# Turning the adjacency on VectorE, by way of DRAM, instead of on TensorE in the first graph stage

## The chip, the cores and the metric

The kernel runs on one core of a Trainium2 chip. A core has five engines with instruction streams of their own: TensorE (PE in the profile) for matrix products, VectorE (DVE), ScalarE (ACT), GpSimd (POOL) and SyncE (SP), which here only issues DMAs. GpSimd issues DMAs too. The metric is the device time of one execution in microseconds, as a median of several runs; the time of a run is somewhat longer than the span that its profile shows.

## The reference

A two-layer graph network on x of 16 batches, 1024 nodes and 256 channels, with one adjacency `adj` of 1024 x 1024 for all batches. All data is float32. Cut to what matters:

```python
# layer 0, per batch; h = relu(layernorm(x)), fea = h transposed
c_adj = mean(fea, channels)
A = abs(abs(sigmoid(c_adj[None, :] - c_adj[:, None]) - 0.5) - 0.5) * 2   # symmetric
g = relu((fea @ (adj * A)) * para)               # "graph product", gives the queries
k, v = split(h @ kv_w)
x = x + softmax(q @ k.T * scale) @ v             # 4 heads of 64 channels
# layer 1; h = relu(layernorm(x))
A_norm = adj + eye
deg = A_norm.sum(0) + A_norm.sum(1) - diag(A_norm)
A_hat = A_norm * rsqrt(deg)[:, None] * rsqrt(deg)[None, :]
agg = A_hat @ h                                  # per batch
x = x + batchnorm(relu(batchnorm(agg @ W1.T + b1)) @ W2.T + b2)
```

Layer 0 reads the adjacency by rows. Layer 1 needs it transposed in the tile `ahatT`, scaled by the roots of the degrees. The transposed copy, the sums and the scaling are made once, while batch 0 is worked on.

## The kernel before

Nodes lie in 8 chunks of 128 partitions. `adj_t[0..7]` hold the rows of the adjacency for the whole run. Work of each engine is issued in the order of the program text, which is written out by hand: functions take lists of small steps ("hooks") that they call at set places, so an instruction's place in the text is its place in its engine's queue, SyncE's and GpSimd's DMA queues included. An engine that waits holds everything queued behind it.

Batch 0 begins with its layer norm. `prepare_row(0)` makes, by transposes on TensorE (L317, L323), a row of node means that is the same on every partition. `weights(b, c)` makes one chunk of masked weights: two activations on ScalarE (L350, L353) from the row, then one operation on VectorE with the adjacency chunk (L367). Weights sit in the pool `w4`, which has five buffers; the graph's parameters, W1 and W2 pass through the same five.

`graph(0, between)` runs over the 8 chunks: it calls the steps of `between[c]`, then multiplies (L489) into two PSUM tiles. At chunk 5 it loads the parameters (L482), whose buffers come free when chunks 3 and 4 have been multiplied. After the last chunk come seven products each for values and keys (`V.product`, `K.product`: a seven-product scheme with sums on VectorE, `add`, and copies on ScalarE, `copy`).

Among these steps stand the adjacency's eight blocks. `turn_adj(i)` and `turn_adj_aside(i)` transpose the eight 128 x 128 pieces of one row chunk on TensorE against the identity into PSUM (L1372, L1387), and `place_adj` copies the result into `ahatT` on VectorE, or once on ScalarE (L1378, L1393). `row_sums` and `column_sums` are activations with an accumulator on ScalarE. `diagonal` takes out the diagonal and adds the identity on GpSimd, 16 small operations, and reduces it on VectorE (L1414).

`prepare_row(b)` for later batches writes the means to DRAM in 4-byte pieces (`frow`, L312) and loads them back broadcast to all partitions (`f_row`, L313), both on SyncE. For batch 1 this is a step at the end of the chunks, `between[8]`.

`attention(0, ...)` then runs four steps. In each, `scores` makes 8 score tiles (L868, three PSUM buffers) with exponentials on ScalarE (L876) and sums on VectorE; before the last sum it calls `hooks[i]`. `partial` and `values` (L920) follow. `hooks[0]` and `hooks[1]` make batch 1's first two chunks of weights; column sums stand in all four hooks, two in each; `roots` in the last. In step 2 `collect`, `invert` and `spread` spread the reciprocals of the softmax's sums. After the attention comes `graph(1, ...)`, whose fourth chunk is preceded by `roots_row`, and then the scaling of `ahatT`. From there on the batches run alike.

[...]

Of the kernel before, what the change touches and what calls it, by code (L numbers as in the profile page):

```python
# [10 lines left out]
F32 = mybir.dt.float32  # L11
# [18 lines left out]
def fast_path(  # L30
# [39 lines left out]
    w2T_d = dram.tile([P, FC, C], F32, tag="fw2T", name="fw2T")  # L70
    w1s_d = dram.tile([P, 4, FC * P // 2], F32, tag="fw1s", name="fw1s")
# [106 lines left out]
    with ExitStack() as stage:  # L178
# [291 lines left out]
        def graph(b, between):  # L470
# [42 lines left out]
            if b == 0:  # L513
# [8 lines left out]
                K.copy(0, 0)  # L522
                V.product(6)
# [9 lines left out]
                K.copy(1, 0)  # L533
                V.product(4)
# [13 lines left out]
                K.copy(0, 1)  # L548
                return qT, kT, v
# [819 lines left out]
        def turn_adj(i):  # L1369
            ps = ps_s.tile([P, NC, P], F32, tag="s", name=f"f_adjps_{i}")  # L1370
            for m in range(NC):
                nc.tensor.transpose(ps[:, m, :], adj_t[i][:, ts(m, P)], ident)  # L1372
            turned_adj[i] = ps

        turned_adj = {}

        def place_adj(i, copy):
            copy(columns(i), turned_adj.pop(i).rearrange("p m (q i) -> p m i q", i=NC))  # L1378

        def turn_adj_aside(i):  # L1380

            turned_adj[i] = [
                ps_o.tile([P, NC // 2, P], F32, tag="o", name=f"f_adjpsa_{i}"),
                ps_t.tile([P, NC // 2, P], F32, tag="t", name=f"f_adjpsb_{i}"),
            ]
            for m in range(NC):
                nc.tensor.transpose(  # L1387
                    turned_adj[i][m // 4][:, m % 4, :], adj_t[i][:, ts(m, P)], ident
                )

        def place_adj_aside(i, copy):
            for n, ps in enumerate(turned_adj.pop(i)):
                copy(columns(i)[:, 4 * n : 4 * n + 4], ps.rearrange("p m (q i) -> p m i q", i=NC))  # L1393
# [14 lines left out]
        def diagonal():  # L1408
# [5 lines left out]
            nc.vector.tensor_reduce(diag, on, AX.X, ALU.add)  # L1414
# [44 lines left out]
        with tc.manual_schedule(engines={ENG.PE, ENG.Activation, ENG.DVE, ENG.Pool, ENG.SP}):  # L1459
# [16 lines left out]
            turn_adj(0)  # L1476
            place_adj(0, nc.vector.tensor_copy)
            xs[1] = load_x(1)
            prepare_row(0)
            turn_adj(1)  # L1480
            turn_adj_aside(2)
            place_adj(1, nc.vector.tensor_copy)
# [5 lines left out]
            def load_w1T():  # L1488
# [6 lines left out]
                    1: [  # L1495
                        lambda: place_adj_aside(2, nc.vector.tensor_copy),
# [39 lines left out]
            for b in range(B):  # L1536

                hooks, aside, behind = {}, {}, None
                if b + 1 < B:
# [9 lines left out]
                    if b == 0:  # L1549
                        for m in range(NC):  # L1550
                            hooks.setdefault(m // 2, []).append(lambda m=m: column_sums(m))
# [985 lines left out]
```

## Time and profile before

| | us |
|---|---|
| median of 3 runs (lowest, highest) | 2359.56 (2359.32, 2362.05) |
| the profiled execution's own time | 2359.85 |
| its span | 2358.1 |
| TensorE busy in the span | 2319.4 |
| VectorE busy | 1994.5 |
| ScalarE busy | 1416.2 |
| GpSimd busy | 447.5 |
| first graph product, start | 16.58 |
| first product of keys and values, start | 48.72 |
| first scores of batch 0, start | 61.07 |
| first graph product of batch 1, start | 117.41 |

A timeline row has a start, a duration, the engine, the line, the operation with the tiles that it writes and reads, and a count when equal instructions are merged; in brackets the idle time of the engine before it and what ended it. A float32 matrix product of 512 columns counts as two matrix instructions. Starts are in microseconds from the start of the span. In the kernel after the change lines are shifted: those behind the new `adjT_d` by 1, those of the attention by 7.

### The profile page before, as it was taken

The page shows a single profiled execution, that of the slowest core. Times are in us where ns is not written, and L with a number is a line of the kernel's source. Part 1 is how long each engine was busy: PE and PEld are TensorE (multiplying, and loading weights), DVE is VectorE, ACT ScalarE, POOL GpSimd, SP SyncE. Part 2 cuts the span into 40 slices and gives each one's busy share as a digit, 9 for nine tenths or more (in the row PEclk, how much of TensorE's full clock was granted, in tenths as well). Part 3 has the DMA queues.
Part 4 walks back from the last instruction along what each step waited for, and adds up shares of the span by engine and source line. Part 5 has one row for each costly group of instructions (what it writes and reads, how often), then busy time and mean ns, then how long its engine had stood idle before and what let it go on. Part 6 is the DMA issues. An engine that isn't in the chain of part 4 may idle for free.

```text
span 2358.1 us, 25774 instructions
## 1 busy us (share of the span) xinstructions
PE 2319.4 (98%) x8256; PEld 1030.5 (44%) x8256; DVE 1994.5 (85%) x2937; ACT 1416.2 (60%) x2057; POOL 447.5 (19%) x573
## 2 busy tenths in 40 slices
PE   8999999999999999999999999999999999999995
PEld 5353444434353434444343434343444434444444
DVE  7988989898989899897989798988989898757766
ACT  6846556574838465655657384746556575346644
POOL 5121212112221112221212221222212121100000
PEclk9999999999999999999999999999999999999998
DMA  6143443524342434335343324253343421355579
GB/s 205 46 143 99 139 138 117 161 107 122 130 138 69 170 96 162 115 134 143 113 132 132 123 86 156 90 179 99 134 143 116 156 77 54 128 215 176 171 243 380
DMA packets 169217, 326.42 MB, mean 138 GB/s; under 512 B 34928, under 2 KB 102000, under 8 KB 169072
## 3 DMA queue, kind: packets, MB, share of 16 engines
q1 hardware_dynamic: 145264, 268.02, 33.3%
q0 software_dynamic: 19200, 39.88, 6.3%
q10 hardware_dynamic: 4608, 16.78, 1.7%
q8 instruction: 67, 1.10, 0.2%
q14 instruction: 78, 0.64, 0.1%
HBM read 203.96 MB, written 101.77 MB: 130 GB/s over the span
## 4 chain that ended last, share of the span: by engine, by line
PE 97%; DMA 1%; DVE 1%; issue 0%; ACT 0%; SPq 0%; ACTq 0%; POOLq 0%; POOL 0%; DVEq 0%
PE f_s L868 19%; PE f_o L920 19%; PE f_aps L1085 16%; PE f_gps L686 8%; PE f_zps L1195 7%; PE f_gpsx L686 6%; PE f_zx L1756 4%; PE f_zm L1756 3%; PE f_gps L489 2%; PE f_vpsx L433 2%; PE f_kpsx L428 2%; PE f_vps L433 2%; PE f_kps L428 2%; PE f_z2ps L1694 1%; PE f_zps L1278 1%; PE f_zps3a L1195 1%
## 5 line engine op out<-in xcount | busy, mean ns | idle before, releaser
L876 ACT ACTIVATE f_p<-f_s 128x1024 f32<-128x1024 f32 x512 | 477.0, 1047 | 59.8 <-PE f_s L868 59.8
L868 PE MATMUL f_s<-f_qT,f_kT 64*128 64x512 f32 x2048 | 456.8, 596 | 0.0
L920 PE MATMUL f_o<-f_p,f_v 128*64 128x512 f32 x2048 | 453.6, 595 | 0.0
L868 PEld LDWEIGHTS f_s<-f_qT,f_kT 64*128 64x128 f32 x2048 | 191.2, 185 | 263.6 <-issue 118.3
L920 PEld LDWEIGHTS f_o<-f_p,f_v 128*64 128x64 f32 x2048 | 141.4, 137 | 304.4 <-issue 265.7
L363 POOL TENSOR_TENSOR f_w<-f_w,f_adj 128x1024 f32<-128x1024 f32 x56 | 132.2, 2362 | 700.9 <-ACT f_w L362 506.7
L988 POOL DMA_DIRECT2D f_att<-f_oT x256 | 136.1, 539 | 342.8 <-DVE f_oT L971 337.3
L891 DVE TENSOR_TENSOR f_acc<-f_acc,f_p 128x1024 f32<-128x1024 f32 x128 | 156.0, 1219 | 4.6 <-ACT f_p L876 4.6
L891 DVE TENSOR_TENSOR f_sums<-f_sums,f_p 128x1024 f32<-128x1024 f32 x128 | 155.9, 1218 | 0.0
L350 ACT ACTIVATE f_w<-f_row,f_col 128x1024 f32<-128x1024 f32 x127 | 147.4, 1160 | 10.9 <-DMA f_row<-frow 4.6
L353 ACT ACTIVATE f_w<-f_w 128x1024 f32<-128x1024 f32 x127 | 134.4, 1058 | 4.0
L1085 PE MATMUL f_aps<-f_ahatT,f_hs 128*128 128x512 f32 x256 | 115.1, 592 | 0.0
L1085 PE MATMUL f_aps<-f_ahatT,f_h_b 128*128 128x512 f32 x256 | 112.6, 593 | 0.0
L1085 PE MATMUL f_aps<-f_t,f_hs 128*128 128x512 f32 x256 | 112.5, 592 | 0.0
L362 ACT ACTIVATE f_w<-f_w,f_now 128x1024 f32<-128x1024 f32 x56 | 64.3, 1148 | 78.9 <-DVE f_now L360 78.9
L686 PE MATMUL f_gps<-f_w,f_h_a 128*128 128x512 f32 x224 | 109.8, 592 | 0.0
L882 DVE TENSOR_TENSOR f_acc<-f_p,f_p 128x1024 f32<-128x1024 f32 x64 | 77.9, 1218 | 24.9 <-ACT f_p L876 24.9
L888 DVE TENSOR_TENSOR f_sums<-f_p,f_p 128x1024 f32<-128x1024 f32 x64 | 78.2, 1221 | 20.2 <-ACT f_p L876 20.1
L367 DVE SCALAR_TENSOR_TENSOR f_w<-f_w,f_adj 128x1024 f32<-128x1024 f32 x71 | 88.0, 1258 | 7.5 <-ACT f_w L353 7.4
L283 ACT ACTIVATE f_h_a<-f_x,f_shift_a,f_rstd_a 128x256 f32<-128x256 f32 x126 | 73.8, 587 | 32.3 <-DVE f_shift_a L268 32.3
L1218 ACT ACTIVATE f_z<-f_zps,f_b 128x512 f32<-128x512 f32 x60 | 38.0, 683 | 75.3 <-PE f_zps L1195 75.3
L283 ACT ACTIVATE f_h_b<-f_x,f_shift_b,f_rstd_b 128x256 f32<-128x256 f32 x128 | 66.2, 592 | 25.8 <-DVE f_shift_b L268 25.8
(297 smaller groups left out, 3984.2 us busy)
## 6 DMA issues: line engine op xcount, KB each, us to landing
f_t<-ft SPq DMA_DIRECT2D x84, 512.0 KB, 9.7
fz<-f_z SPq DMA_DIRECT2D x64, 512.0 KB, 9.5
f_x<-in_x_dram SPq DMA_DIRECT2D x31, 1024.0 KB, 6.2
f_zb<-fz SPq DMA_DIRECT2D x42, 512.0 KB, 4.6
fx<-f_x SPq DMA_DIRECT2D x16, 1024.0 KB, 4.4
fgs<-f_gs POOLq DMA_DIRECT2D x28, 512.0 KB, 3.0
fhT<-f_hQ POOLq DMA_DIRECT2D x112, 128.0 KB, 3.2
f_hT<-fhT SPq DMA_DIRECT2D x28, 512.0 KB, 6.4
```

What stands on the lines that cost most here:

```text
L283: nc.scalar.activation(self.h[:, c, :], self.xt[:, c, :], AF.Relu, bias=self.shift[:, c : c + 1], scale=self.rstd[:, c : c + 1], accum_out ...
L350: nc.scalar.activation(w, rows[b], AF.Abs, bias=cols[b][:, c : c + 1], scale=0.5 / C)
L353: nc.scalar.activation(w, w, AF.Tanh)
L686: nc.tensor.matmul(ps, left, right, start=fresh and n == 0, stop=(n == PAIRS - 1), skip_group_check=more,)
L868: nc.tensor.matmul(ps[:, e, :], kT[rows_e, pair, ts(m, P)], qT[rows_e, pair, ts(g, 512)], start=True, stop=True,)
L876: nc.scalar.activation(p, ps, AF.Exp)
L891: nc.vector.tensor_add(to, to, p)
L920: nc.tensor.matmul(o_of[s][e * HD : (e + 1) * HD, :], v[:, m, ts(2 * pair + e, HD)], p[:, e, :], start=(m == 0), stop=(m == NC - 1),)
L988: queue.dma_start(t[ts(j, 32), :, a].rearrange("r h c i -> r h (c i)"), oT[ts(a, 32), :, j].rearrange("r h c i -> r h (c i)"),)
L1085: nc.tensor.matmul(ps, left[:, m, :], right(m), start=not more and m == 0, stop=(m == KH - 1), skip_group_check=more,)
L1195: nc.tensor.matmul(ps[i], left[:, ts(i, P)], right, start=not more, stop=True, skip_group_check=more,)
L1756: nc.tensor.matmul(ps, left[:, m, :], right[:, m, :], start=start and m == 0, stop=(m == 1), skip_group_check=not start,)
```

## The change

The transposes on TensorE and the copies out of PSUM go. The adjacency is loaded a second time, its rows sorted so that VectorE's transposition of 32 x 32 blocks, done on eight tiles of 128 x 1024, leaves in `ahatT` (as a staging area) pieces that eight stores from GpSimd's queue put in DRAM as the transposed matrix (`adjT_d`, pieces of 512 bytes). Four loads of 1 MB bring it back into `ahatT`.

The 32 loads of 128 KB are on SyncE: twelve after the parameters (`load_adj_ahead`, into tiles of the attention that are not in use yet), twenty after the last chunk (`load_adj_behind`, into the five buffers of `w4`). VectorE's eight transposes are called among the key and value products, at three new places "first", "then" and "end". The batch's row moves from `between[8]` to "first", so that on SyncE it comes after all the loads. The diagonal follows the reload; its reduction moves into the last hook. Row sums are spread out: three in the chunks, three among the keys and values, two in hook 0. Column sums move into hooks 2 and 3, four in each. Chunk 5's weights are made one step earlier.

```diff
@@ graph(b, between), keys and values of batch 0
                 K.copy(0, 0)
+                for step in between["first"]:
+                    step()
                 V.product(6)
...
                 K.copy(1, 0)
+                for step in between["then"]:
+                    step()
                 V.product(4)
...
                 K.copy(0, 1)
+                for step in between["end"]:
+                    step()
                 return qT, kT, v
@@
-        def turn_adj(i):
-            ps = ps_s.tile([P, NC, P], F32, tag="s", name=f"f_adjps_{i}")
-            for m in range(NC):
-                nc.tensor.transpose(ps[:, m, :], adj_t[i][:, ts(m, P)], ident)
-            turned_adj[i] = ps
...
+        stage_rows = ahatT.rearrange("p m x -> p (m x)").rearrange("p (k t r) -> p k t r", k=32, t=NC)
+        by_rows = adj.rearrange("(u i) d -> i u d", i=NC)
...
+        def load_adj(t, home):
+
+            pool, tag, bufs = home
+            to = pool.tile([P, N], F32, tag=tag, name=f"f_adjr_{t}", bufs=bufs)
+            for a in range(4):
+                nc.sync.dma_start(to[ts(a, 32)], by_rows[2 * a + t // 4, ts(t % 4, 32)])
+            adj_rows[t] = to
+
+        def load_adj_ahead():
+            for t, home in enumerate(((ow, "oT", 2), (ow, "oT", 2), (ow, "att", 1))):
+                load_adj(t, home)
+
+        def load_adj_behind():
+            for t in range(3, NC):
+                load_adj(t, (w4, "w4", 5))
+
+        def turn_adj(t):
+            nc.vector.transpose(
+                stage_rows[:, :, t], adj_rows.pop(t).rearrange("p (k s) -> p k s", s=32)
+            )
+
+        def store_adj(half):
+
+            to = adjT_d.rearrange("(k s) (a g x) -> g a s k x", s=32, a=4, g=2)[half]
+            for a in range(4):
+                nc.gpsimd.dma_start(
+                    to[a],
+                    stage_rows[ts(a, 32), :, 4 * half : 4 * half + 4].rearrange(
+                        "p k t r -> p k (t r)"
+                    ),
                 )
...
+        def reload_adj():
+            whole = adjT_d.rearrange("(m p) x -> p m x", p=P)
+            for m in range(0, NC, 2):
+                nc.sync.dma_start(ahatT[:, m : m + 2], whole[:, m : m + 2])
@@ the steps of graph(0), new
                     0: [lambda: weights(0, 2), lambda: turn_h(0)],
+                    1: [lambda: weights(0, 3)],
                     2: [
                         lambda: weights(0, 4),
+                        lambda: weights(0, 5),
                         lambda: turn_weights(w1n, unused("w1Q"), w1T_d, FC),
                         lambda: prepare_start(1),
                     ],
+                    3: [lambda: weights(0, 6)],
+                    4: [lambda: weights(0, 7), *(lambda m=m: row_sums(m) for m in range(3))],
                     6: [
+                        load_adj_ahead,
                         lambda: prepare_end(1),
                         make_key_sums,
                         load_w1T,
                         lambda: again(0),
                     ],
-                    8: [lambda: prepare_row(1)],
+                    8: [load_adj_behind],
+                    "first": [
+                        lambda: turn_adj(0),
+                        lambda: turn_adj(1),
+                        lambda: prepare_row(1),
+                        lambda: row_sums(3),
+                    ],
+                    "then": [
+                        lambda: turn_adj(2),
+                        lambda: turn_adj(3),
+                        lambda: store_adj(0),
+                        lambda: row_sums(4),
+                        lambda: row_sums(5),
+                    ],
+                    "end": [
+                        *(lambda t=t: turn_adj(t) for t in range(4, NC)),
+                        lambda: store_adj(1),
+                    ],
@@ ahead of the attention, and its hooks
-            diagonal()
+            reload_adj()
+            sum_diagonal = diagonal()
...
-                            hooks.setdefault(m // 2, []).append(lambda m=m: column_sums(m))
+                            hooks.setdefault(2 + m // 4, []).append(lambda m=m: column_sums(m))
+                        hooks[0].extend((lambda: row_sums(6), lambda: row_sums(7)))
+                        hooks[3].append(sum_diagonal)
```

## The prediction

> **What bounds the kernel now.** I read the page first, then the timeline of each engine over the first 130 us, because the diff ends there: from the second graph stage on both programs issue the same work.
>
> The first two lines are from the page: busy time of TensorE (PE), and the chain of work that ended last.
>
> ```profile
> PE 2319.4 (98%) x8256; PEld 1030.5 (44%) x8256; DVE 1994.5 (85%) x2937; ACT 1416.2 (60%) x2057; POOL 447.5 (19%) x573
> ...
> PE 97%; DMA 1%; DVE 1%; issue 0%; ACT 0%; SPq 0%; ACTq 0%; POOLq 0%; POOL 0%; DVEq 0%
> ```
>
> So every microsecond taken from TensorE counts, and every microsecond that TensorE is made to wait counts. Next, TensorE's timeline of the stage (start, us, engine, line, operation):
>
> ```profile
> 12.65 1.91 PE L323 MATMUL f_rps<-f_ident,f_sums 128*128 128x128 f32 x8
> 14.36 1.43 PE L1372 MATMUL f_adjps<-f_ident,f_adj 128*128 128x128 f32 x8
> ...
> 16.58 3.67 PE L489 MATMUL f_gps<-f_w,f_h_a 128*128 128x512 f32 x8
> 20.09 1.04 PE L1372 MATMUL f_adjps<-f_ident,f_adj 128*128 128x128 f32 x8
> 20.96 3.60 PE L489 MATMUL f_gps<-f_w,f_h_a 128*128 128x512 f32 x8
> ...
> 38.42 10.46 PE L489 MATMUL f_gps<-f_w,f_h_a 128*128 128x512 f32 x24
> 48.72 1.05 PE L433 MATMUL f_vpsx<-f_kvw,f_hT 128*128 128x128 f32 x8
> ```
>
> A chunk of the graph product is eight matrix instructions of 0.43 us, 3.44 us. Between chunks stand the transposes of the adjacency, and there is no gap: 16.58 to 48.72 is 32.14 us, of which eight chunks are 27.5.
>
> Then the SyncE queue, ScalarE (ACT) at the first attention hook, and the page's DMA rows (queue, count, KB, median us from issue to landing):
>
> ```profile
> 46.22 0.57 SPq L312 DMA_DIRECT2D frow<-f_sums  x1
> 59.28 0.33 SPq L313 DMA_DIRECT2D f_row<-frow  x1
> ```
> ```profile
> 69.56 1.21 ACT L350 ACTIVATE f_w<-f_row,f_col 128x1024 f32<-128x1024 f32 x1
> ...
> 76.33 4.69 ACT L876 ACTIVATE f_p<-f_s 128x1024 f32<-128x1024 f32 x5 [2.40 <-PE f_s L868]
> ```
> ```profile
> f_row<-frow SPq DMA_DIRECT2D x15, 512.0 KB, 4.8
> ...
> frow<-f_sums SPq DMA_DIRECT2D x15, 4.0 KB, 10.3
> ```
>
> The row of node means for batch 1 goes through DRAM: 4 KB in 4-byte pieces, 13.1 us here, then a broadcast load of 4.5. It is used at 69.56, some 5 us after landing, and ScalarE then has 2.40 us to spare before the next exponentials.
>
> Last, VectorE (DVE) beside GpSimd (POOL), and at the end of the attention:
>
> ```profile
> L455 DVE TENSOR_TENSOR f_kt<-f_hT,f_hT x15: 683/686/1006, 43.2 to 1950.2; 128x512 f32<-128x512 f32 x15
> ```
> ```profile
> 102.76 1.02 ACT L962 COPY f_recs<-f_rec 32x32 f32<-32x32 f32 x4 [1.68 <-DVE f_rec L954]
> ...
> 104.56 1.94 ACT L876 ACTIVATE f_p<-f_s 128x1024 f32<-128x1024 f32 x2 [0.78 <-PE f_s L868]
> ```
>
> The 1006 ns (of min, median, max) is the one of fifteen that ran while the diagonal's small operations were on GpSimd.
>
> **The change part by part.** I count from T, TensorE's first product of keys and values (48.72 before).
>
> *Removed from TensorE: 64 transposes.* In the loop the blocks cost, from each block's start to the next chunk's, 0.87, 1.09, 0.88, 0.88 and 0.88: **-4.6**. The chunks then stand back to back; ScalarE needs 2.2 us for a chunk's weights and VectorE 1.2, against 3.44, and moving weights 5 forward keeps them ahead. The 24 transposes ahead of the loop stood in waits. Without them the first broadcast copy of the row (L317) ends some 0.5 earlier, the second at 14.3 rather than 14.56, and VectorE's first masked half and the first chunk follow: **-0.3**. VectorE also loses 8.9 us of copies out of PSUM (four of 1.22, six of 0.67) and ScalarE one of 0.99.
>
> *The clock at the start: +2.4[...].* Eight transposes took 1.9 us up to 14.5 and 1.04 from 20.09, so TensorE's rate doubled, by the block at 14.36 to 15.6 around 15.2, after some six busy microseconds. That is in the durations; the granted-clock column of these early windows shows 1.00 throughout. [...] here the rate doubled when nothing but transposes had run, so I go by the trace. After the change TensorE is busy only from about 11.6 to 14.3 and idle until 16.3; [...] I take 2.4; 0 if the shorter burst is enough. The first chunks are on the path, with nothing to hide this.
>
> *SyncE: 32 loads of 128 KB, 4 reloads of 1 MB; frow moved behind 20 of the loads.* Loads like them (w2n) are issued every 0.47 us. The second parameter load still waits for chunk 4, T-10.1; twelve loads follow to about T-4, then fkvs, w1T and x, then twenty to about T+8: 2.5 MB of them and 2 MB of the others at the 370 GB/s of the x load. With a stall or two of 1.2 in SyncE's queue, as the trace has, frow is issued at about T+9 instead of T-2.5. Its DRAM write needs 8.6 to 13.1 us in all fifteen cases. The windows show no byte moved between 52 and 58 while it was awaited, so it is the completion that is slow. [...] By the row: T+9, +10.4, +0.4, +6 for the broadcast beside the stores = T+25.8. ScalarE wants it at T+20.8 and has 2.4 to spare, so the deadline is T+23.2: **+3.0**, between 0 (issue T+8.3, write 8.6, load 4.5: T+21.8) and 8.7 (T+31.9). Behind that waiting activation stand two row sums and all exponentials of the second attention step; TensorE fills its three score banks and waits. Behind frow's wait on SyncE stand the row, w2n and the reloads.
>
> *VectorE: eight transposes.* None of this shape is in the trace; turn_h's pair takes 2.36 and w1's 1.24, so 1.2 each, 9.6 in all. Two after the first V sum (T+2.7 to 5.2), two before V.add(1,0,4) (to T+10.1), four after the last K sum (T+12.7 to 17.6). The sums that free PSUM banks still come ahead of TensorE, and the first attention sums move from T+15.6 to T+17.6. The cover is the o transpose, T+30.4 against T+33.5 when TensorE wants the bank: 0. If the last load landed 4 us later it would cost about 1.
>
> *ScalarE:* three row sums of 1.05 between the key and value copies, with the last copy ready 0.2 ahead of K.product(3), and the queries' relus 0.8 later: **+0.3**, between 0 and 1. Four column sums in step 2 instead of two end at 103.1 in the old times, before spread is due: 0.
>
> *GpSimd: 8 stores, then the diagonal, both later.* The first four stores follow T+10, the others T+17.6; 512 descriptors cost 0.74 us to issue and 256 cost 0.62, so 1.0 each. 4 MB in 512-byte pieces at 200 GB/s or so land by T+31. Reloading starts at about T+32, after w2n, and ends at T+46; the 16 operations of the diagonal run from T+37 to T+48. Column sums of chunks 0 to 3 are due at T+50 plus the stall above: 0, with 5 us of cover; beyond that each microsecond costs one.
>
> *VectorE beside the diagonal: +2.2, between 0 and 4.* Before, the 16 operations cost VectorE about 3.0 (make_key_sums 1.4, h_sums 1.2, two small ones 0.4) where it had room. Now they fall into attention steps 1 and 2, where it is busy for 18.9 and 19.7 us of 20. About 2 of lag reaches invert; spread waits for it with 0.78 to spare: 1.2. The diagonal's reduction, 1.21, moves from T+12.6 into step 3, ahead of batch 1's third weights, which have 1.05 to spare: about 1 more. Lower end 0, because masked_aside's operations (L363) hardly slow the same sums; upper end if none is caught up.
>
> **Sum:** -4.6 - 0.3 + 2.4 + 3.0 + 0.3 + 2.2 = +3.0 on the profiled execution's 2359.85 us (span 2358.1): 2362.85. It stands 0.29 above the median of the runs, so the forecast is **2362.6 us**.
>
> **The rivals.**
> - *The row comes late [...]: clearly slower.* Stores (4 MB) share engines with frow and the broadcast. From a row at T+28 on, the stall is over 5; [...] With 6 to 9 in place of 3: +6 to +11, near 2368. For: frow already took 13.1 behind one large load. Against: it took 8.6 to 11 in most cases beside stores.
> - *The round trip comes late: slower.* If 512-byte stores run at 100 GB/s, the reload ends at T+64, and column sums hold up step 3's exponentials by about 8 more: 2371. Against: w1T's stores kept up with their issue.
> - *Everything is covered: faster.* Row by T+23, [...] VectorE catches up: about -3, 2356.5. -4.9 is the floor.
> - *Nothing saved because the transposes were hidden* is excluded by the gapless loop.
>
> **How the numbers follow.** Forecast case 0.48; late row 0.30; late round trip 0.10; all covered 0.12. About 0.2% (4.7 us) is what a measurement of this kernel can tell from no change. The floor is just past it: 0.04 faster. Of the forecast case 0.06 lies above it, and 0.08 of the covered case lies within: same 0.50; slower 0.46. The range 2357.5 to 2370 leaves out about 0.08 of the covered case and 0.10 at the top.
>
> **What would show it.** The loop's chunks without transposes, T earlier by about 2.5 and not 4.9, with the first chunk's instructions near 0.85 us; the first attention hook (L351 there) waiting for frow's load, and TensorE idle ahead of the second step's scores; then short waits at spread and at batch 1's third chunk. A row that lands before T+23, a first chunk at full rate, or column sums waiting for GpSimd would prove me wrong in that step.

## The result: 0.9% slower, and the profile after

The changed kernel takes 2381.38 us (median of 6 runs, 2376.62 to 2382.01) against 2360.07 for the kernel before (6 runs, 2359.32 to 2362.05): a ratio of 1.0086, 95% interval 1.0075 to 1.0097. The forecast was 2362.6, with a range up to 2370. The profiled execution is the quickest of the six, 2376.62 us with a span of 2374.8; the other runs' 2.5 to 5.4 us more have no profile, but in e7 below, whose order of work is the same, the two steps that lose most take 4.5 us longer together than here.

The page first: TensorE's busy time has grown by 3 us although 64 transposes are gone, and the chain that ended last is no longer TensorE to 97%.

```profile
PE 2322.6 (98%) x8192; PEld 1024.2 (43%) x8192; DVE 1995.3 (84%) x2935; ACT 1416.0 (60%) x2056; POOL 460.5 (19%) x581
...
PE 93%; DMA 2%; DVE 2%; ACT 1%; issue 1%; SPq 1%; POOL 0%; DVEq 0%; ACTq 0%; POOLq 0%
```

TensorE's timeline of the changed kernel (start, us, engine, line, operation, and in brackets the wait before it):

```profile
16.41 29.84 PE L490 MATMUL f_gps<-f_w,f_h_a 128*128 128x512 f32 x64 [1.92 <-DVE f_w L337]
...
46.09 1.05 PE L434 MATMUL f_vpsx<-f_kvw,f_hT 128*128 128x128 f32 x8
...
56.53 1.12 PE L429 MATMUL f_kps<-f_kt,f_kvs 128*128 128x512 f32 x2 [0.59 <-ACT f_v L444]
...
60.04 7.14 PE L875 MATMUL f_s<-f_qT,f_kT 64*128 64x512 f32 x32 [0.68 <-ACT f_kT L444]
...
79.32 1.98 PE L927 MATMUL f_o<-f_p,f_v 128*64 128x512 f32 x4 [5.98 <-ACT f_p L883]
81.23 4.97 PE L875 MATMUL f_s<-f_qT,f_kT 64*128 64x512 f32 x12
90.57 7.13 PE L875 MATMUL f_s<-f_qT,f_kT 64*128 64x512 f32 x20 [4.38 <-ACT f_p L883]
```

The loop is as forecast: one row of 64, and T (the first product of keys and values) at 46.09 instead of 48.72, 2.6 earlier. Everything is lost behind it. The table is made of the starts of such rows: the loop up to T, keys and values up to the first scores, each attention step from its scores to the next, and the start of batch 1's graph product. I use it for all kernels below.

| kernel | loop | T | K and V | step 0 | step 1 | step 2 | step 3 | batch 1's graph |
|---|---|---|---|---|---|---|---|---|
| before | 32.14 | 48.72 | 12.35 | 14.09 | 14.08 | 14.09 | 14.08 | 117.41 |
| after | 29.68 | 46.09 | 13.95 | 21.19 | 23.42 | 14.08 | 14.30 | 133.03 |
| difference | -2.46 | -2.63 | +1.60 | +7.10 | +9.34 | 0 | +0.22 | +15.62 |

The span is 16.7 longer, so the first attention holds nearly all of it. Two waits do it. SyncE's timeline and ScalarE's and VectorE's at the two places:

```profile
36.39 7.12 SPq L1385 DMA_DIRECT2D f_adjr<-in_adj_dram  x12
...
45.69 20.32 SPq L1385 DMA_DIRECT2D f_adjr<-in_adj_dram  x20
66.05 2.06 SPq L313 DMA_DIRECT2D frow<-f_sums  x1
78.50 0.34 SPq L314 DMA_DIRECT2D f_row<-frow  x1
...
92.14 2.09 SPq L1415 DMA_DIRECT2D f_ahatT<-fadjT  x4
```
```profile
75.80 1.25 DVE L1397 STREAM_TRANSPOSE f_ahatT<-f_adjr 128x1024 f32<-128x1024 f32 x1 [9.25 <-DMA f_adjr<-in_adj_dram]
76.97 1.18 DVE L889 TENSOR_TENSOR f_acc<-f_p,f_p 128x1024 f32<-128x1024 f32 x1
```
```profile
78.25 1.02 ACT L883 ACTIVATE f_p<-f_s 128x1024 f32<-128x1024 f32 x1 [10.44 <-DVE f_acc L889]
85.30 1.15 ACT L351 ACTIVATE f_w<-f_row,f_col 128x1024 f32<-128x1024 f32 x1 [6.03 <-DMA f_row<-frow]
...
119.16 1.02 ACT L969 COPY f_recs<-f_rec 32x32 f32<-32x32 f32 x4 [0.60 <-DVE f_rec L961]
```

Twenty loads take 20.3 us to issue, up to T+20, not T+8. VectorE's last transpose waits 9.25 us for its load. Behind it stands the first sum of the attention, which frees a tile of eight that the eighth exponential needs, because the diagonal's product now holds one of the others until step 3. So ScalarE waits 10.44 and TensorE 5.98 in step 0. Then the row: issued at 66.05, awaited until 78.50, used at 85.30, which is T+39. Of the 9.34 us that step 1 loses, TensorE waits 4.38; the other 5.0 are its 32 score products, which take 12.1 us (4.97 and 7.13) in place of 7.14. The reload and the column sums cost no wait; and of the former spare time at `spread` the wait of 1.68 is now 0.60.

The page's DMA rows (queue, count, KB, median us to landing) and four stretches of 4 us (the last three columns are the granted clock, the DMA engines' busy share and GB/s):

```profile
f_row<-frow SPq DMA_DIRECT2D x15, 512.0 KB, 4.8
f_adjr<-in_adj_dram SPq DMA_DIRECT2D x32, 128.0 KB, 5.4
fadjT<-f_ahatT POOLq DMA_DIRECT2D x8, 512.0 KB, 9.5
...
frow<-f_sums SPq DMA_DIRECT2D x15, 4.0 KB, 10.1
```
```profile
42.00:46.00 4.00, 4.00 (x10) 1.71 (x9) 1.23 (x1) 0.00 (x0) 0.00 (x0) 1.00 1.04 249
...
62.00:66.00 4.00, 4.00 (x22) 1.59 (x18) 1.56 (x2) 4.00 (x6) 0.00 (x0) 1.00 1.02 215
...
74.00:78.00 4.00, 0.00 (x0) 0.00 (x0) 2.20 (x2) 0.00 (x0) 0.66 (x1) 1.00 0.00 0
...
82.00:86.00 4.00, 4.00 (x12) 1.34 (x8) 1.83 (x2) 0.70 (x1) 0.00 (x0) 0.56 0.98 298
```

The engines are full (1.04, 1.02) at 215 to 249 GB/s, not at the 370 that the forecast took. From 74 to 78 nothing moves at all: only the completion of `frow` is awaited, and TensorE stands still. The granted clock, 1.00 up to 74, is 0.56 from 82 to 86 and 0.50 from 90 to 94, and step 1's score products lie just there: the first 12 take 4.97 us, where 32 take 7.14 in step 0.

### The profile page after: what moved, and what is told of

The parts are those of the page before. It is cut to its first block, busy times and chain, and to the rows that moved or that the text cites. A ratio compares the mean times of both kernels' runs of the same rounds, so it can differ in the third digit from the quotient of the medians.

```text
span 2374.8 us, 25722 instructions
## 1 busy us (share of the span) xinstructions
PE 2322.6 (98%) x8192; PEld 1024.2 (43%) x8192; DVE 1995.3 (84%) x2935; ACT 1416.0 (60%) x2056; POOL 460.5 (19%) x581
## 4 chain that ended last, share of the span: by engine, by line
PE 93%; DMA 2%; DVE 2%; ACT 1%; issue 1%; SPq 1%; POOL 0%; DVEq 0%; ACTq 0%; POOLq 0%
PE f_s L875 18%; PE f_o L927 17%; PE f_aps L1092 16%; PE f_gps L693 8%; PE f_zps L1202 7%; PE f_gpsx L693 6%; PE f_zx L1774 4%; PE f_zm L1774 3%; PE f_gps L490 2%; PE f_vpsx L434 2%; PE f_kpsx L429 2%; PE f_vps L434 2%; PE f_kps L429 2%; PE f_outps L1994 1%; PE f_zps L1285 1%
## 5 line engine op out<-in xcount | busy, mean ns | idle before, releaser
L875 PE MATMUL f_s<-f_qT,f_kT 64*128 64x512 f32 x2048 | 462.2, 601 | 5.0 <-ACT f_p L883 4.4
L284 ACT ACTIVATE f_h_b<-f_x,f_shift_b,f_rstd_b 128x256 f32<-128x256 f32 x128 | 66.2, 592 | 25.8 <-DVE f_shift_b L269 25.8
```

Source lines behind the costliest of these rows:

```text
L284: nc.scalar.activation(self.h[:, c, :], self.xt[:, c, :], AF.Relu, bias=self.shift[:, c : c + 1], scale=self.rstd[:, c : c + 1], accum_out ...
L875: nc.tensor.matmul(ps[:, e, :], kT[rows_e, pair, ts(m, P)], qT[rows_e, pair, ts(g, 512)], start=True, stop=True,)
```

## The experiments

Theory after the traces: the loads land late, and two things behind them (the row on SyncE's queue, the sums on VectorE) hold up the attention. The rivals changed with the results; the runs are told by what they ask, which is not always the order in which they were made. Ratios are to the kernel before on the same chip.

### Moving single parts: e1 to e4

e1 moves batch 1's row to GpSimd's queue, ahead of the twenty loads:

```diff
-                nc.sync.dma_start(row_d[b]..., sums_of[b])
-                nc.sync.dma_start(row, row_d[b]...)
+                queue = nc.gpsimd if b == 1 else nc.sync
+                queue.dma_start(row_d[b]..., sums_of[b])
+                queue.dma_start(row, row_d[b]...)
...
-                    8: [load_adj_behind],
+                    8: [lambda: prepare_row(1), load_adj_behind],
```


> Edit: for batch 1 alone the row's write and its broadcast load are issued by GpSimd, ahead of the twenty loads. Theory 'two waits, row last': in the changed kernel the last adjacency load holds VectorE until 75.8 us, and after that the row (landed 85.3) holds ScalarE until the exponentials of step 1 at 89.5. With the row at hand by about 62 only the first wait is left: exponentials of step 1 start near 83.6, 6 us earlier, and the kernel loses 6 of the 21 us (about 2375). Rival 'the row is the whole cost': all of it goes, about 2362. Rival 'the row is hidden behind the late load': nothing, about 2381.

e2 gives the diagonal's product a tile of its own, and reduces it a step earlier:

```diff
-            on = unused("d").rearrange("p (m q) -> p m q", q=P)
+            on = ow.tile([P, NC, P], F32, tag="att", name="f_diag_on", bufs=1)
...
-                        hooks[3].append(sum_diagonal)
+                        hooks[2].append(sum_diagonal)
```


> Edit: the diagonal's product lies in the tile of the attention's spread output instead of in one of the eight tiles of the exponentials, and is reduced in hook 2. Theory: in the changed kernel the eighth exponential of step 0 waits for VectorE (10.4 us, TensorE idle 5.98) because the diagonal's product keeps one of the eight tiles. With eight tiles free that wait goes, step 0 takes about 15 us instead of 21, but the exponentials of step 1 still wait for the row at 85.3: TensorE idles there instead, and the time stays within 1 us of 2381. Rival 'the tile is what costs': 6 us less, about 2375.

e3 does both, e4 moves the 1 MB reload of x (`again(0)`) from chunk 6 to behind the reload of the turned adjacency.

> Both edits of the two kernels before. Theory: the row is early and the eighth tile free, so only the reuse of the first tile by step 1 is left, which waits for VectorE's first sum behind the last adjacency load (78.2 in the changed kernel): exponentials of step 1 near 78.5, 11 us earlier, about 2370. Rival 'VectorE's lag is absorbed': about 2364. Rival 'row alone matters': the same as the row's edit alone.

> Edit: the 1 MB load of x (again(0)) is issued after the reload instead of ahead of the twenty adjacency loads. Theory 'SyncE's loads are held by x': one load waited from 50.5 to 55.4 for the semaphore of x, which landed 10.6 us after its issue. Without it the twenty loads end some 8 us sooner (frow issued near 57 instead of 66), the last one lands before 66, VectorE is not late, the row lands near 75, and exponentials of step 1 start near 79: 10 us less, about 2371. Rival 'the loads themselves are slow (250 GB/s, engines busy)': the data still has to pass, frow is issued near 63, 3 us less, about 2378.

| kernel | us (median) | ratio, 95% interval | K and V | step 0 | step 1 | step 3 | batch 1's graph |
|---|---|---|---|---|---|---|---|
| e1 row on GpSimd | 2379.16 | 1.0083 (1.0067 to 1.0100) | 13.96 | 27.65 | 15.36 | 19.14 | 136.79 |
| e2 own tile | 2379.57 | 1.0082 (1.0065 to 1.0098) | 13.96 | 23.61 | 25.14 | 14.89 | 137.72 |
| e3 both | 2380.10 | 1.0086 (1.0070 to 1.0103) | 13.95 | 23.62 | 17.12 | 20.88 | 135.62 |
| e4 x late | 2377.57 | 1.0073 (1.0057 to 1.0090) | 13.95 | 14.09 | 34.48 | 14.08 | 138.16 |

Each did what its edit says: in e1 the row's write was through at 55.9 instead of 78.5, in e2 no exponential waited for VectorE's sum, in e4 step 0 lost nothing. And each lost the same again elsewhere: in e1 and e3 the twenty loads took 30.0 and 26.2 us to issue instead of 20.3, and in e4 the write of the row took 17 us instead of 12.4. The expectations of some 2375 for e1, 2370 for e3 and 2371 for e4 fell. e2 stayed near its 2381, but not in the expected way: step 0 took 23.61 instead of about 15, TensorE waiting some 1.2 us for an exponential before each of four groups of score products, for which I have no cause. What moves from place to place must lie under all of them, in the transfers.

### Which transfers: e5, e6, e10

Three kernels leave out a part of the transfers; their texts say which.

> Leaves out the turning of the adjacency: no second load, no VectorE transpose, no store; the four reloads bring the adjacency as it lies, so the values are those of a matrix that was not turned. Everything else (no transposes on TensorE, row sums among keys and values, reduction of the diagonal late, row of batch 1 through SyncE) is as after. Theory (the loss of 21 us is the slow second load and what stands behind it): first product of keys and values at 46.1 as after, row of batch 1 back by 62, no stall of TensorE over 1 us in attention steps 0 and 1, total 2357 to 2359, a little faster than before. Rival (the loss comes from the held tile, the row sums and the moved copies, the load only shows it): 2365 or more.

> Keeps the 32 loads and the eight VectorE transposes; leaves out the eight stores to DRAM, and the four reloads bring the adjacency as it lies. Theory A (the stores share the DMA engines with the loads and with the row's 4-byte writes and slow both): twenty loads issued in 12 us or less instead of 20.3, row back by 70 instead of 79 to 84, total 2365 to 2370. Theory B (the loads are slow by themselves, by 4 KB rows into 32 partitions): twenty loads still need 17 us or more, the last transpose still waits for its load, total within 4 us of after (2377 to 2382).

> Leaves out the second load alone: VectorE turns the tiles that are already there, so the rows come unsorted; eight stores, four reloads and everything else as after. Theory A (the sum of bytes sets the pace, and loads or stores alone fit): no stall over 1 us at row, eighth exponential or column sums, total 2357 to 2360. Theory B (the stores hold up the row's 4-byte writes by themselves): row used 5 us late or more, total 2364 to 2370.

```diff
# e5; e6 has only the cuts in store_adj and reload_adj
         def load_adj(t, home):
+            return
         def turn_adj(t):
+            return
         def store_adj(half):
+            return
         def reload_adj():
-            whole = adjT_d.rearrange("(m p) x -> p m x", p=P)
+            whole = adj.rearrange("(m p) x -> p m x", p=P)
# e10: no loads; VectorE turns what is there
         def load_adj(t, home):
+            return
...
-                stage_rows[:, :, t], adj_rows.pop(t).rearrange("p (k s) -> p k s", s=32)
+                stage_rows[:, :, t], adj_t[t].rearrange("p (k s) -> p k s", s=32)
```

| kernel | us (median) | ratio, 95% interval | T | K and V | step 0 | step 1 | step 3 | batch 1's graph |
|---|---|---|---|---|---|---|---|---|
| e5 neither loads nor stores | 2358.65 | 0.9993 (0.9985 to 1.0002) | 45.51 | 12.36 | 14.08 | 14.09 | 14.09 | 114.21 |
| e10 no loads | 2360.25 | 1.0003 (0.9994 to 1.0011) | 46.19 | 13.21 | 14.08 | 14.09 | 15.72 | 117.37 |
| e6 no stores | 2366.18 | 1.0027 (1.0015 to 1.0038) | 43.80 | 13.96 | 14.68 | 22.64 | 14.08 | 123.25 |

e5 came out as expected, within 2357 to 2359, and its rival is out: the held tile, the row sums and the moved copies cost nothing by themselves. VectorE's transposes and the stores cost 1.6 (e10 over e5), the transposes and the loads 7.5 (e6 over e5), all together 22.7 (after over e5): 13.6 more than the sum. They share the engines: in after, from 62 to 66, the queue of the stores took 88.9% of the 16 engines' time and that of the loads 13.3%. With the stores the twenty loads take 20.3 us to issue, without them (e6) 13.9, and the later loads hold up the row and VectorE for longer. For e6 theory A holds, two thirds of the loss went with the stores; but 13.9 is not under 12, so B has a part in it. For e10 theory A holds as well, but for 1.6 us in step 3, to which I come back.

e10 is worth a second look: it is the forecast's sum without the row, -4.6 - 0.3 + 2.4 + 0.3 + 2.2 = 0.0. It measured +0.5 in the median and -0.04 at the start of batch 1's graph product. The total is closer than its terms: in this profile the first chunk started 0.43 later, not 0.3 earlier, keys and values took 0.86 more and step 3 1.64 more.

### Why the loads are slow: e7 and e18

e7 takes 32 neighbouring rows at a time, e18 one transfer of 128 neighbouring rows in place of four of 32 partitions; in both the rows come unsorted.

```diff
# e7
-                nc.sync.dma_start(to[ts(a, 32)], by_rows[2 * a + t // 4, ts(t % 4, 32)])
+                nc.sync.dma_start(to[ts(a, 32)], adj[ts(4 * t + a, 32)])
# e18
-            for a in range(4):
-                nc.sync.dma_start(to[ts(a, 32)], by_rows[2 * a + t // 4, ts(t % 4, 32)])
+            nc.sync.dma_start(to, adj[ts(t, P)])
```


> The second load takes 32 neighbouring rows at a time (one run of 128 KB of DRAM) instead of every eighth row: the same bytes, pieces and partitions, so the rows come unsorted. Theory A (the stride of 32 KB in DRAM makes the loads slow): 350 GB/s or more while they run, twenty loads issued in 12 us or less, total 2365 or below. Theory B (the target of 32 partitions, or the load of the engines by stores and x, sets the pace): as after, 240 to 270 GB/s, total 2377 to 2382.

> As after, but each of the eight tiles is loaded by one transfer of 128 neighbouring rows (512 KB, all 128 partitions) instead of four of 32 partitions; the same bytes and 4 KB pieces, rows unsorted. Theory (transfers of 32 partitions run at 60% of the rate of those of 128, as the reloads at 400 GB/s against the loads at 250 suggest): over 330 GB/s while they run, loads landed by 62 instead of 76, total 2362 to 2372. Rival (the mixture of streams, or the reading side, sets the pace): 240 to 290 GB/s, total 2376 to 2382.

e7: 2380.97 us, ratio 1.0086 (1.0071 to 1.0102), as after; where the rows lie in DRAM is not it. e18: **2364.22 us, 1.0019 (1.0012 to 1.0026)**, 17 us less than after with the same bytes. Windows of e7 (first fence) and e18:

```profile
42.00:46.00 4.00, 4.00 (x10) 1.71 (x9) 0.78 (x2) 0.23 (x2) 0.00 (x0) 1.00 0.91 220
...
58.00:62.00 4.00, 3.32 (x12) 1.31 (x12) 4.00 (x6) 2.29 (x3) 2.82 (x4) 1.00 1.02 254
```
```profile
46.00:50.00 4.00, 4.00 (x24) 2.80 (x23) 2.88 (x4) 0.58 (x1) 0.00 (x0) 1.00 1.05 389
50.00:54.00 4.00, 4.00 (x28) 3.27 (x28) 3.52 (x5) 2.54 (x5) 0.00 (x0) 1.00 1.05 406
```

With the engines equally full, transfers over all 128 partitions move 389 to 406 GB/s, those over 32 partitions 220 to 254. Why that is so no trace shows. The stores are of 32 partitions too. At the 215 to 249 GB/s of after's full windows above, 4.2 MB of loads and the first 2.1 MB of stores take 25 to 29 us; 2.6 MB of x, parameters, fkvs and w1T at the 370 of before's load of x take another 7. Begun at 36.4 that ends at 69 to 73, an estimate, and the last load was there at 75.8. The forecast had the last one issued at T+8, which is 54.

e18 changes the number and size of the transfers along with their width. In after x was issued at 44.87 and seven loads behind it by 50.85; the eighth waited 4.6 us, until 55.45, for x to land. If eight transfers of a queue can be in flight, as that wait suggests, they hold up to 4 MB in e18 instead of 1 MB, and with only five loads behind x none has to wait for it. That the engines are full in both speaks against this rival, and e4, where that wait is gone, gained little; but no run changes the width alone, so the width as the cause is argued, not shown.

SyncE's timeline of e18: the row leaves at T+2.6 (T is 47.18), and is used at 74.39, T+27.2; the forecast had T+25.8. Step 1 takes 18.44, +4.4 where +3.0 was forecast, and step 0 nothing. So with loads at the rate that it assumed the forecast of 2362.6 is off by 1.6, but in part by luck: the row left 6.4 us earlier than the forecast's T+9, and its write took 16.6 us in place of 10.4.

```profile
42.98 6.77 SPq L1384 DMA_DIRECT2D f_adjr<-in_adj_dram  x5
49.80 0.43 SPq L313 DMA_DIRECT2D frow<-f_sums  x1
66.44 0.33 SPq L314 DMA_DIRECT2D f_row<-frow  x1
```

### Spreading the loads: e8 and e11

e8 issues the loads in the loop: 12 ahead of it, 20 at its first chunk, into tiles that are free there.

> The whole change with the second load issued in the first graph stage: 12 loads ahead of the loop, 20 at its first chunk, into tiles that are free there; VectorE turns blocks 0 to 2 beside chunks 3 to 5, blocks 3 to 5 at the end of the loop, 6 and 7 after the first sum of the values; the stores follow each half. Theory (the loss is the time at which the slow loads land, not the way through DRAM): all loads landed by 48, row of batch 1 issued by 50 and back by 66, stalls of TensorE in attention steps 0 and 1 below 2 us together, total 2357 to 2361. Rival 1 (loads in the loop hold up x, hT or the parameters, and the loop waits): chunks of the loop with waits of 2 us or more, total 2362 or more. Rival 2 (round trip and held tile cost by themselves): 2365 or more with the row in time.

2378.92 us, ratio 1.0080 (1.0066 to 1.0094), and the reason is rival 1: the parameters stand behind the loads on SyncE, are issued at 55.27, and TensorE waits 17.64 us among keys and values. The expected 2357 to 2361 fell. From there on the four steps take 14.08, 14.09, 14.08 and 14.57, and TensorE waits for no load and no row; but the 17.64 us gave the transfers that much more time, so this proves little.

e11 puts this right: 8 loads ahead of the loop, 24 behind the parameters, x late as in e4, row and tile as in e3.

```diff
+            load_adj_ahead()                        # tiles 0 and 1, ahead of the loop
             qkv = graph(
...
-                        load_adj_ahead,
+                        load_adj_behind,            # tiles 2 to 7, at chunk 6
...
-                    8: [load_adj_behind],
+                    8: [lambda: prepare_row(1)],    # on GpSimd's queue
```


> The whole change with its transfers spread out: 8 of the 32 loads ahead of the loop, 24 after the parameters at chunk 6; the reload of x behind the turned adjacency; the row of batch 1 on GpSimd's queue ahead of the stores; the diagonal's product in a tile of its own. Theory (bytes against time, one queue, one held tile; nothing else): loads landed by 55, row by 58, stalls of TensorE in attention steps 0 and 1 under 1.5 us together, total 2357.5 to 2360.5. Rival (each move only shifts the stall, as in the runs with the row and the tile moved): some wait of 3 us or more stays before the first attention step ends, total 2364 or more.

2367.47 us, 1.0032 (1.0020 to 1.0043): the rival. Keys and values take 22.56, with one wait of 7.29 for a sum that stands behind `turn_adj(3)` to `turn_adj(5)`, whose loads VectorE awaits for 6.00 and 1.02. The windows of 2 us show what the loads were doing while `frow` was written (issued at 43.9, through by 56.4):

```profile
46.00:48.00 2.00, 2.00 (x15) 1.63 (x14) 1.49 (x2) 0.35 (x1) 0.00 (x0) 1.00 1.27 228
48.00:50.00 2.00, 2.00 (x15) 1.52 (x14) 1.39 (x2) 0.83 (x3) 0.00 (x0) 1.00 1.50 122
50.00:52.00 2.00, 2.00 (x15) 1.52 (x14) 0.45 (x1) 1.51 (x3) 0.00 (x0) 1.00 0.27 10
52.00:54.00 2.00, 2.00 (x15) 1.52 (x14) 0.00 (x0) 0.79 (x2) 0.00 (x0) 1.00 0.93 29
54.00:56.00 2.00, 2.00 (x16) 1.57 (x15) 0.00 (x0) 0.38 (x1) 0.00 (x0) 1.00 0.46 33
```

10 to 33 GB/s for 6 us, with loads issued and waiting. e1 has the same in its windows (29, 37 and 41 GB/s from 48 to 54). So the row of 4 KB stops the loads of megabytes.

### The row's pieces: e13 and e14

e13 is after with one edit: a small transpose on TensorE turns the sums and ScalarE copies them out, so that the write has 8 pieces of 512 bytes instead of 1024 of 4. e14 is the same edit in e11.

```diff
+                if b == 1:
+                    turned = ps_t.tile([P, 512], F32, tag="t", name="f_rowps_1")
+                    nc.tensor.transpose(turned[:NC, :P], sums_of[b], ident)
+                    flat = row[:NC, :P]
+                    nc.scalar.copy(flat, turned[:NC, :P])
+                    nc.sync.dma_start(row_d[b].rearrange("(c p) -> c p", p=P), flat)
+                else:
                     nc.sync.dma_start(row_d[b].rearrange("(c p) -> p c", p=P), sums_of[b])
```


> As after, in after's order, but the sums of batch 1 are turned by one small transpose on TensorE and copied by ScalarE, so that their write to DRAM has 8 pieces of 512 bytes instead of 1024 of 4 bytes; the row's values are the same. Theory (the 12 us of this write are its small pieces): it lands within 4 us of issue, the first attention hook stops waiting for the row or waits under 1 us instead of 6.0, total 2371 to 2376. Rival (the write is slow because it stands behind 20 loads and the stores): it still takes 10 us or more, total 2378 to 2382.

> e11_spread with the sums of batch 1 written in 8 pieces of 512 bytes. Theory (while the 1024 pieces were written, 48 to 56 us, the loads moved 10 to 33 GB/s; that is why each earlier place of the row cost what it brought): the loads keep over 200 GB/s there, all landed by 60, the wait of 7.3 us among keys and values falls below 1.5, total 2358.5 to 2361.5. Rival (the loads stop there for another reason, such as full queues): waits as in e11_spread, total 2366 to 2369.

e13: 2369.21 us, 1.0040 (1.0025 to 1.0056), 12 less than after in the medians, 2 better than expected. On its SyncE the row's load can be issued 7.9 us after the write, where it was 12.4 (the 2.06 of issue in both is the queue behind the loads), so the "4 us" missed; ScalarE still waits 2.14 before it uses the row, instead of 6.03 (the profile names w2n's load, issued next to the row's, as what ended this wait).

```profile
66.95 2.06 SPq L318 DMA_DIRECT2D frow<-f_row  x1
74.88 0.36 SPq L321 DMA_DIRECT2D f_row<-frow  x1
```

Step 1 falls from 23.42 (30.89 in e7) to 17.19; step 0 keeps 4.4 of its 7.1, since its cause, the late load, stays. e14: 2361.00 us, 1.0008 (0.9999 to 1.0016). The same stretch of its windows; over 200 GB/s was expected, and it is 196 to 238:

```profile
48.00:50.00 2.00, 2.00 (x15) 1.52 (x14) 1.39 (x2) 0.83 (x3) 0.00 (x0) 1.00 1.05 238
50.00:52.00 2.00, 2.00 (x15) 1.52 (x14) 1.58 (x2) 1.50 (x3) 0.06 (x1) 1.00 0.82 196
52.00:54.00 2.00, 2.00 (x15) 1.52 (x14) 1.74 (x3) 0.79 (x2) 2.00 (x3) 1.00 0.96 238
```

Keys and values fall from 22.56 to 13.37. With nothing else changed, this is shown: 1024 pieces of 4 bytes made the write itself slow (12.4 us against 7.9 in its old place, and 4.6 in e14 against 12.5 in e11) and stopped the loads beside it. That e1 and e3 gained nothing fits this; neither was run with the 8 pieces.

### The other terms: e9, e12, e15, e16, e17

e9 is e5 with eight transposes ahead of the loop, from `adj_t[0]` into a bank that nobody reads; e12, e15 and e17 are e11, e14 and e16 with the same.

```diff
             prepare_row(0)
+            ps = ps_s.tile([P, NC, P], F32, tag="s", name="f_warm_0")
+            for m in range(NC):
+                nc.tensor.transpose(ps[:, m, :], adj_t[0][:, ts(m, P)], ident)
```


> The kernel of e5_direct (no second load, no VectorE transpose, no store; the adjacency is brought as it lies) with eight transposes of the first adjacency tile put back on TensorE ahead of the loop, into a bank that nobody reads. Theory (the burst before the idle 1.9 us is too short to bring the rate up safely, and 0 to 3.2 us of the first chunks run at half rate by chance): the 64 products of the loop take 27.5 to 27.8 us in the profile instead of 29.35, total about 1.5 to 2.5 under e5_direct, 2356.2 to 2357.2, with a smaller spread of its runs. Rival (the slow first chunks are a matter of operands that come late, not of the clock): 29 us or more and the same total as e5_direct.

> e11_spread with eight transposes of the first adjacency tile put back ahead of the loop, into a bank that nobody reads. Theory: 1.5 to 2.5 under e11_spread, so about 2356 to 2358.5, and the 64 products of the loop in 27.5 to 27.8 us. Rival: no difference from e11_spread.

> e14_spread_row with eight transposes of the first adjacency tile ahead of the loop, into a bank that nobody reads. Theory: the 64 products of the loop in 27.5 to 27.8 us and 1.5 to 2.7 under e14_spread_row: 2356.5 to 2359, the fastest version with the whole work done. Rival: within 0.5 of e14_spread_row.

e9: 2356.01 us, 0.9984 (0.9977 to 0.9990), 2.64 below e5. TensorE's timeline:

```profile
14.07 1.91 PE L1498 MATMUL f_warm<-f_ident,f_adj 128*128 128x128 f32 x8
16.28 27.70 PE L490 MATMUL f_gps<-f_w,f_h_a 128*128 128x512 f32 x64 [0.30 <-DVE f_w L337]
```

In all four kernels with these transposes the loop's products take 27.5 to 27.7; in the 15 others with the changed loop, after among them, 27.6 (e6) to 30.6, although TensorE does the same work ahead of it. In after the loop's weight loads, one ahead of each product, start 0.85 us apart from 17.42 to 19.98 and 0.43 apart from 20.77 on. So 0.1 to 3.1 us are lost at the start, by chance as far as the traces show; with the eight transposes it is 0.0 to 0.2.

But the gain need not reach the end. e12: 2366.74, 1.0032 (1.0019 to 1.0044), with T 3.0 earlier than in e11 in the profiles and only 0.7 gained in the median. e15: 2362.55, 1.0012 (1.0006 to 1.0019), 1.6 above e14, with a spread of 2358.6 to 2366.0. Its T is 2.9 earlier than e14's, but its reload is issued no earlier (82.08 against 81.17); GpSimd's products for the diagonal follow the reload, VectorE's reduction of them starts at 102.02 (101.33), and the reciprocals behind that reach ScalarE at 105.63 (104.93), so that TensorE waits 4.21 us in step 3. Where the transfers set the pace, an earlier T is only a longer wait.

e16 takes the diagonal's products from the adjacency as first loaded, during the loop, so that eight operations on GpSimd are left behind the reload instead of 16, and their reduction on VectorE moves from step 2 to among keys and values; e17 adds the transposes.

```diff
+        def diagonal_product():
+            on = unused("d").rearrange("p (m q) -> p m q", q=P)
+            for m in range(NC):
+                nc.gpsimd.tensor_mul(on[:, m, :], adj_t[m][:, ts(m, P)], ident)
+            return lambda: nc.vector.tensor_reduce(diag, on, AX.X, ALU.add)
...
         def diagonal():
...
-                nc.gpsimd.tensor_mul(as_columns(on[:, m, :]), block, as_columns(ident))
                 nc.gpsimd.tensor_add(block, block, as_columns(ident))
```


> e14_spread_row with the diagonal's eight products taken from the adjacency as first loaded, on GpSimd during the loop, and their reduction on VectorE among keys and values; only the eight additions of the identity stay behind the reload. Theory (what is left of e14's loss is VectorE slowed beside GpSimd's 16 operations: 2.0 us of waiting at batch 1's weights in attention step 3): the wait falls below 1, total 2358.5 to 2360.5. Rival (VectorE is late there for its own work): the wait stays at 2 or more, total as e14.

> e16_spread_diag with eight transposes of the first adjacency tile ahead of the loop, into a bank that nobody reads. Theory A (terms add): 1.5 to 2.7 under e16_spread_diag, 2356.5 to 2358.5, below the kernel before. Theory B (with TensorE 2.7 earlier, the transfers set the end, as e15 against e14 suggests): within 1 of e16_spread_diag, with longer waits for the last load or the reload.

Step 3 of e14 took 16.63, with this wait in TensorE's timeline:

```profile
107.05 4.79 PE L883 MATMUL f_s<-f_qT,f_kT 64*128 64x512 f32 x20 [2.03 <-ACT f_p L891]
```

In e16 and e17 step 3 takes 14.09 and the wait is gone; whether by the fewer operations or by the earlier reduction is not told apart. e16: 2358.81 us, 0.9997 (0.9988 to 1.0005). e17: **2357.98 us, 0.9994 (0.9986 to 1.0002)**, 0.8 below e16 although T is 2.0 earlier: theory B by the medians. But the two profiles still differ by 1.65 at batch 1's graph product, so the longer waits that B expected are not seen there, and where the rest goes is open. It is the best kernel with the whole work done, 1.5 us under the kernel before in the medians, which the interval doesn't tell from no change.

## Why the prediction was wrong, point by point

- **The transposes, -4.6 and -0.3: right.** The first chunk starts 0.17 earlier, and the loop has no gaps.
- **The clock, +2.4: right, the size in part by luck.** 29.68 - 27.5 = 2.2 here, and 2.64 by e9 against e5; but e6 lost 0.1 and e18 3.1 with the same work on TensorE ahead of the loop. The 2.4 itself was an estimate of mine: before shows that the rate doubled after transposes, not how far a shorter burst of them goes. That the removed transposes bear on the rate was rightly read from that trace: with eight of them put back ahead of the loop (e9) its products take 27.70 us, without (e5) 29.35.
- **SyncE's loads, at 370 GB/s: the step that failed.** In after's two full windows above they and the stores moved 215 to 249, over 32 partitions; with loads of 128 partitions (e18) 17 of the 21 us go. That is no share that adds up with others: the row's pieces alone give back 12 (e13), because a faster load also lets the row leave earlier. The rate was that of the load of x (370 GB/s from 48 to 50 in before), which goes to 128 partitions. Stores (at "200 GB/s or so") were put beside the loads as if each had the engines to itself; e5, e6 and e10 show that 13.6 us come from their being there together.
- **The row, +3.0 (0 to 8.7): +9.3 measured, out of its bounds, for the issue at T+20 in place of T+9.** By the forecast's own figures the term was 25.8 - 23.2 = 2.6, not 3.0, which changes nothing here. Its 10.4 for the write was near 12.4, but in e18 the write took 16.6. That the write slows the loads was not thought of. The rival of the late row has nearly this size (6 to 9), but got its lateness from the stores on the row's own way; and 5.0 of the 9.3 lie in products at a granted clock of 0.56 and 0.50.
- **VectorE's transposes, 0: +7.1.** "If the last load landed 4 us later it would cost about 1": it was awaited until T+29.7; the forecast had the last four transposes from T+12.7 on. Overlooked was the diagonal's tile, one of eight, held until step 3. It costs only together with a late load: step 0 loses nothing in e5 (no load) and e18 (last load by 65.6), and 4.4 in e13 (awaited until 73.8, in after until 75.8).
- **ScalarE's row sums, +0.3 (0 to 1): 0.0 in e5.** With VectorE's transposes among the sums keys and values take 0.9 more (e10), with late loads 1.6.
- **The round trip, 0: right.** Column sums at 114.30 wait for nothing; the rival that feared it is out.
- **VectorE beside the diagonal, +2.2 (0 to 4): 0.9 here** (0.22 in step 3, 0.67 at batch 1's third chunk). Where the attention is not stopped before and the reduction stands as in after, it is 2.3 (e10: 1.64 and 0.67), as forecast. In e14, with the reduction in step 2 and 0.90 of waiting for GpSimd ahead of it, step 3 takes 2.5 more, and in e16 nothing more.

The range up to 2370 let the row and the round trip fail one at a time. It had no case in which one cause, the pace of the transfers, moves several terms at once.

## What to carry to other kernels

Sum the bytes of a stretch over all queues, take for each transfer a rate measured on one of its own kind (here the width in partitions, with which e18 changed the size), and only then ask when each lands; two transfers that fit alone need not fit together. Where an early step only moves a wait, stop moving steps and take the transfers out one by one: three such runs said more here than four moves. A small write in 4-byte pieces is no small transfer: turned into 8 pieces, it gave back 12 us in e13 and made the difference between 2367 and 2361 in e14.

## What the runs showed of the hardware that I had not expected

- Transfers of 32 partitions with DMA engines 91% busy or more: 215 to 268 GB/s in stretches of 4 us (after, e7); of 128 partitions: 389 to 406 from 46 to 54 (e18). The stride of the rows in DRAM made no difference (2380.97 us in e7, 2381.38 in after).
- While 1024 pieces of 4 bytes were written, loads on another queue fell to 10 to 41 GB/s for about 6 us (e11, e1), and in e18 loads and stores together to 83 and 71 GB/s over 8 us. With 8 pieces of 512 bytes they kept 196 to 238 (e14).
- The half rate at the start of the loop (0.85 us a product in after, then 0.43) cost between 0.1 and 3.1 us from kernel to kernel with the same instructions ahead of it on TensorE; eight transposes more, ending 0.3 to 1.1 us before the first product, left 0.0 to 0.2 of it.
